# Products of the states with C, shared between VectorE and GpSimd in a fused state-space and attention kernel

## The chip, the cores and the metric

The kernel runs on one core of one Trainium2 chip. The metric is the device time of one launch in microseconds, as the median of several runs. A core has five engines that run side by side, each through its own instructions in order: TensorE (PE, matrix products), VectorE (DVE), ScalarE (ACT), GpSimd (POOL) and SyncE (SP). SP issues most of the DMAs; POOL issues those that add to what is there (`accum_op`), between its own arithmetic. The engines wait for one another by semaphores only.

## What is computed

Two layers over x of shape (2, 768, 64, 64), all in float32; the change lies in the first. Cut to what matters:

```python
xs = conv3x3_depthwise(in_proj(groupnorm(x)))        # 1536 channels, 9 taps
u = silu(xs)
dt, Bs, Cs = split(x_proj(u))                        # 48, 4 and 4 values a position
delta = softplus(dt_proj(dt) + dt_b)
dA  = exp(delta[..., None] * A)                      # 4 states a channel
dBu = (delta * u)[..., None] * Bs
s_t = dA_t * s_(t-1) + dBu_t                         # along all 4096 positions
y = sum_n(s_n * Cs_n) + D * u
out = out_proj(layernorm(y)); x = x + out
# second layer: attention over channels by heads, with two 768 x 768 products
```

## The kernel before, in words

The first layer works on tiles of 512 positions (8 rows of 64) by 128 channels: 16 tiles of positions (`NI`) with 12 chunks of channels each (`KI`), 192 pieces (`NQ0`), counted by g. The program is one loop over `step(g)`, in an order written out by hand (`tc.manual_schedule`); what stands first in a step's text is first in its engine's queue. One step works on several pieces at once: the input projection of piece n = g + 17, the convolution taps of piece a = g + 15 (`AHEAD`), the scan of piece g, the first sums of piece g - 1, the squares of g - 3, the output projection of the tile before (`BEHIND` = 12). A short fill comes before step 0, and the second layer (Strassen products and attention) after the last step.

The nine taps of the convolution are shared out. The middle one is ACT's (`tap_act`, line 412: it starts the sum `acc` in PSUM). `DMA_TAPS` (line 49) names those that ACT scales into `tm` buffers (line 427) and POOL's DMAs add up: `taps_dma_sum(a, q)` (line 433) adds the q-th buffer to the first, `taps_dma(a)` (line 439) adds the first to `u`. `PE_TAPS` (line 50) names those of TensorE, products with a diagonal matrix that ACT makes (`diag`, line 409; `taps_pe`, line 447). Both tuples are indexed by a % 4. What is left is DVE's (`taps_dve`, line 461): it reads the image from SBUF and `acc` from PSUM, and the last tap writes `u`.

For the scan of piece g, ACT makes `delta` for two pieces at a time, at odd g for g + 1 and g + 2 (`softplus_pair`, line 509), and four exponentials into `das[g % 2]` (`exps`, line 514). POOL multiplies delta by u (`du`, line 518, two buffers). DVE multiplies it by B for all four states into the single buffer `s` (line 537), runs the recurrence over the four states at once (line 539) and multiplies the states by C back into `das[g % 2]` (`times_c`, line 546). In the next step POOL adds states 0, 1 to states 2, 3 (`sum1`, line 526), and two DMAs add the two sums to `u`: `y_dma(g, 0)` one step after the scan, `y_dma(g, 1)` two steps after (line 533). ACT has by then multiplied u by D (line 530).

So a step in DVE's queue is: taps of a, product with B, scan, product with C. In POOL's queue it is: `sum1(g - 1)`, `du(g)`, the second tap sum of a, the two y DMAs, the tap sum of a + 1 and the tap DMA of a, and in one step of four two residual DMAs (`out_residual`, line 623). DVE also evicts the output projection in one step of four (line 615).

Of the kernel before, what the change touches and what calls it, by code (L numbers as in the profile page):

```python
# [19 lines left out]
NS = 4  # L20
# [14 lines left out]
NQ0 = NI * KI  # L35
# [11 lines left out]


DMA_TAPS = ((0, 2, 6), (0, 2, 6), (0, 2, 6), (0, 2))
PE_TAPS = ((), (1,), (), (1, 7))  # L50
FILL_DMA_TAPS = (0, 2)

AHEAD = 15
# [14 lines left out]
def both_layers(  # L68
# [225 lines left out]
    us, deltas, dus, sqs, tms = {}, {}, {}, {}, {}  # L294
# [90 lines left out]
    def dma_taps(a):  # L385
        return DMA_TAPS[a % 4] if a >= AHEAD else FILL_DMA_TAPS if a != KI - 1 else ()

    def pe_taps(a):
        return PE_TAPS[a % 4] if a > AHEAD else ()

# [41 lines left out]
    def taps_dma_sum(a, q):  # L432
        nc.gpsimd.dma_start(tms[a][0], tms[a][q], accum_op=ALU.add)  # L433
        if a < AHEAD:
            give(tms[a][q])

    def taps_dma(a):
        tm = tms.pop(a)[0]
        nc.gpsimd.dma_start(us[a], tm, accum_op=ALU.add)  # L439
        if a < AHEAD:  # L440
            give(tm)
# [52 lines left out]
    def load_bc(i, h):  # L494
        nc.sync.dma_start(bc[:, h * NS : (h + 1) * NS, :], bc_dr[i][h * NS : (h + 1) * NS, :].partition_broadcast(P))
# [15 lines left out]
    def exps(g):  # L511
        c = g % KI
        for n in range(NS):
            nc.scalar.activation(das[g % 2][:, n, 1:], deltas[g], AF.Exp, scale=neg_a[:, c, n : n + 1])  # L514

    def du(g):
        dus[g] = wk.tile([P, TL], F32, tag="du", name=f"du{g}")
        nc.gpsimd.tensor_mul(dus[g], deltas.pop(g), us[g])  # L518


    def ysums(g, n):
# [2 lines left out]
    def sum1(g):  # L524
        da = das[g % 2]
        nc.gpsimd.tensor_add(ysum[:, 0 : 2 + g % 2 : 1 + g % 2, :], da[:, 0:2, 1:], da[:, 2:4, 1:])  # L526
# [5 lines left out]
    def y_dma(g, n):  # L532
        nc.gpsimd.dma_start(us[g], ysums(g, n), accum_op=ALU.add)  # L533
# [8 lines left out]
        i, c, b, t = where(g)  # L542
        nc.scalar.copy(s[:, :, 0], state[c] if t else zeros[:, :NS])

    def times_c(g):
        nc.vector.tensor_mul(das[g % 2][:, :, 1:], s[:, :, 1:], bc[:, NS:, :])  # L546

    def state_out(g):
        i, c, b, t = where(g)
# [4 lines left out]
    def square(g):  # L554
        sqs[g] = wk.tile([P, TL], F32, tag="sq", name=f"sq{g}", bufs=3)
        nc.scalar.activation(sqs[g], us[g], AF.Square)
# [239 lines left out]
    lo, hi = slice(0, NH), slice(NH, QL)  # L796
# [358 lines left out]
    with tc.manual_schedule():  # L1155
# [31 lines left out]
        def step(g, prep=None, acts=None):  # L1187
            a, n = g + AHEAD, g + AHEAD + 2
            v = n
            do_b, do_c = 0 <= g < NQ0, BEHIND <= g < NQ0 + BEHIND  # L1190
# [95 lines left out]
            if 0 <= g - 3 < NQ0:  # L1286
                square(g - 3)

            if 0 <= g - 1 < NQ0:
                sum1(g - 1)  # L1290
            if do_b:
                du(g)
            late_tap = 0 <= a < NQ0 and len(dma_taps(a)) > 2
            if late_tap:
                taps_dma_sum(a, 2)
            if 0 <= g - 1 < NQ0:
                y_dma(g - 1, 0)
            if 0 <= g - 2 < NQ0:
                y_dma(g - 2, 1)
            if 0 <= a < NQ0 and dma_taps(a) and not late_tap:  # L1300
                taps_dma(a)
            if 0 <= a + 1 < NQ0 and dma_taps(a + 1):
                taps_dma_sum(a + 1, 1)
            if late_tap:
                taps_dma(a)
            if BEHIND < g <= NQ0 + BEHIND and (g - BEHIND) % 4 == 0:
                out_residual(g)
            if do_b:
# [11 lines left out]
            if 0 <= g + 1 < NQ0:  # L1320
                exps(g + 1)
            if do_b:
                state_out(g)
            if do_b:
                times_c(g)
                if g % KI == KI - 1 and g + 1 < NQ0:
                    load_bc(g // KI + 1, 1)
            if 0 <= g + 1 < NQ0:
# [24 lines left out]
        with tc.tile_pool(name="l0st", bufs=1, side="right") as sp:  # L1353
# [25 lines left out]
            for v in range(AHEAD + 1):  # L1379
                if 2 <= v < 6:  # L1380
                    out_weights_load(wg, 3 * (v - 2))
                step(first + v, lambda: products_of(v), lambda: scalar_of(v))
                if v == 0:
                    nc.scalar.activation(neg_a, pc[:, :, PC_A : PC_A + NS], AF.Exp)
                    nc.scalar.mul(neg_a, neg_a, -1.0)
                for k in scaled_w.get(v, ((), ()))[0]:
                    out_weights_sub(wg, wmean, k, nc.gpsimd)
                for k in scaled_w.get(v - 1, ((), ()))[1]:
                    out_weights_sub(wg, wmean, k, nc.vector)
                for k in sum(scaled_w.get(v - 1, ((), ())), ()):  # L1390
                    out_weights_store(wg, k)
# [8 lines left out]
        bc = late.tile([P, 2 * NS, TL], F32, name="bc")  # L1400
        s = late.tile([P, NS, TL + 1], F32, name="s")
# [4 lines left out]
        das = [late.tile([P, NS, TL + 1], F32, name="da0"), da1]  # L1406
        nc.gpsimd.memset(das[0][:, :, 0], 0.0)
        step(-1)
        nc.gpsimd.memset(das[1][:, :, 0], 0.0)
        for g in range(NQ0 + 2):  # L1410
            step(g)
# [68 lines left out]
@with_exitstack  # L1480
def mamba_then_attention(
    ctx, tc, x, in_wP, xp_wP, dt_wP, out_wT, pc_in, comb_in, pick_in, xsum_in, qkvP, woutP, temp_c, ident_in, gavg_in, gsel_in, hcol_in, hsel_in, esel_in, out
):
    nc = tc.nc
    keep = ctx.enter_context(tc.tile_pool(name="keep", bufs=1))
    dram = ctx.enter_context(tc.tile_pool(name="dram", bufs=1, space=DRAM))
    x1 = [dram.tile([DM, L], F32, name=f"x1_{b}") for b in range(NB)]

    stats1 = [keep.tile([P, KM, 2 * NT + 1], F32, name=f"stats1_{b}") for b in range(NB)]

    ident = keep.tile([P, P], F32, name="ident")
    nc.sync.dma_start(ident, ident_in)
    ones = keep.tile([P, P], F32, name="ones")
    nc.vector.memset(ones, 1.0)
    eps_c = keep.tile([P, 1], F32, name="eps_c")
    nc.vector.memset(eps_c, EPS)
    consts = (ident, ones, eps_c)


    wo_dr = dram.tile([KM // 2, KI // 3, P, 3, 2 * P], F32, name="wo_dr")  # L1500
    bc_dr = [dram.tile([2 * NS, TL], F32, name=f"bc_dr{i}") for i in range(NI)]

    s_dr = {k: dram.tile([KM // 2, 4, P, KM // 2, P], F32, name=f"s_dr_{k}") for k in ("p1", "p3")}
    both_layers(
        tc, nc, consts, x, in_wP, xp_wP, dt_wP, out_wT, pc_in, comb_in, pick_in, xsum_in, gavg_in, gsel_in, wo_dr, bc_dr, s_dr, x1, stats1,
        qkvP, woutP, temp_c, hcol_in, hsel_in, esel_in, [out[b].rearrange("c h w -> c (h w)") for b in range(NB)],
    )
# [105 lines left out]
```

## Time and profile before

| | us |
|---|---|
| median of three runs (3704.88 to 3710.76) | 3709.35 |
| span of the profiled execution | 3708.1 |
| PE busy in it | 3555.3 (96%) |
| DVE busy | 2842.1 (77%) |
| ACT busy | 2571.8 (69%) |
| POOL busy | 1782.8 (48%) |
| scan of one piece, L539, 192 times | 4.433 each, 851.1 in all |
| product with B, L537, 192 times | 2.288 each, 439.2 in all |
| DVE's taps, L461, 890 times | 0.753 and 0.748 each, 669.2 in all |
| delta times u, L518, 192 times | 1.284 each, 246.5 in all |
| PE's taps and their like, L447, 264 records | 140.0 in all |

The first scan starts 193.2 us into the span and the last at 2702.0, so a step takes 13.1 us on the average. The share of a whole span is an average over stages: DVE and ACT have little to do after 2700 us. PE does a product of 128x128 by 128x512 in float32 as two records. Lines of the profile carry the line of the kernel's text, the engine, the operation, the tile written and those read; in groups, the number after "x" is how often, then follow busy us, mean ns of one, and the engine's idle time just before them with what ended it. In answers in order of time the first two numbers are start and length in us.

### The profile page before, as it was taken

How to read it: one execution, taken by the hardware profiler on the slowest of the kernel's cores; microseconds unless marked ns; L12 is line 12 of the kernel's file. 1: busy time of each engine (PE TensorE's matmuls, PEld its weight loads, DVE VectorE, ACT ScalarE, POOL GpSimd, SP SyncE). 2: the span in 40 equal slices, each digit the busy share in tenths (PEclk: the TensorE clock that was granted, in tenths of full speed). 3: DMA queues.
4: the chain of work that ended last, by engine and by line, in shares of the span. 5: the costliest groups of instructions: out<-in, count | busy, mean ns of one | idle time of the engine just before them, and what ended most of it. 6: DMA issues, size and time to landing. Idle time of an engine off the chain costs nothing. (4 is left out here: it accounts for less than half of the span.)

```text
span 3708.1 us, 37935 instructions
## 1 busy us (share of the span) xinstructions
PE 3555.3 (96%) x11176; PEld 1771.0 (48%) x11176; DVE 2842.1 (77%) x2571; ACT 2571.8 (69%) x5026; POOL 1782.8 (48%) x1813
## 2 busy tenths in 40 slices
PE   5968999999999999999999999999999999999999
PEld 3423333343333333333344333433347658886688
DVE  7899999999999999999999999997721362224522
ACT  2688889888988898888888988897633542244221
POOL 0355565565655655555556655654443313330232
PEclk9978999999999999999999999999999999999999
DMA  9877888998989899898898989997676538763487
GB/s 354 232 169 162 182 204 185 205 211 191 212 176 209 201 200 208 184 204 185 187 203 194 212 175 211 203 201 177 142 202 183 192 93 265 256 205 123 158 268 245
DMA packets 380301, 738.98 MB, mean 199 GB/s; under 512 B 44304, under 2 KB 116944, under 8 KB 376000
## 3 DMA queue, kind: packets, MB, share of 16 engines
q0 software_dynamic: 146208, 270.08, 42.6%
q1 hardware_dynamic: 233888, 466.49, 38.4%
q8 instruction: 90, 1.47, 0.2%
q14 instruction: 115, 0.94, 0.1%
HBM read 440.96 MB, written 60.03 MB: 135 GB/s over the span
## 5 line engine op out<-in xcount | busy, mean ns | idle before, releaser
L362 PE MATMUL pa<-u,w 128*128 128x512 f32 (+1 forms) x2304 | 1035.8, 599 | 7.5 <-ACT carry L377 7.3
L603 PE MATMUL po<-u,w 128*128 128x512 f32 x2256 | 1011.5, 598 | 8.1 <-DVE u L615 7.9
L539 DVE TENSOR_TENSOR_SCAN s<-da,s 128x2052 f32<-128x2052 f32 x192 | 851.1, 4433 | 19.5 <-DVE s L537 0.9
L362 PEld LDWEIGHTS pa<-u,w 128*128 128x128 f32 x2304 | 429.5, 192 | 597.7 <-issue 484.7
L603 PEld LDWEIGHTS po<-u,w 128*128 128x128 f32 x2256 | 420.8, 190 | 582.7 <-issue 551.3
L526 POOL TENSOR_TENSOR ysum<-da 128x1024 f32<-128x1024 f32 x192 | 386.8, 2015 | 547.4 <-DVE da L546 464.1
L461 DVE SCALAR_TENSOR_TENSOR acc<-xs,pc,acc 128x512 f32<-128x512 f32 x698 | 525.6, 753 | 29.2 <-ACT acc L415 12.7
L537 DVE TENSOR_TENSOR s<-du,bc 128x2048 f32<-128x2048 f32 x192 | 439.2, 2288 | 83.0 <-POOL du L518 73.8
L433 POOL DMA_DIRECT2D tm<-tm x309 | 270.3, 875 | 462.7 <-ACT tm L427 423.5
L514 ACT ACTIVATE da<-dl,neg_a 128x512 f32<-128x512 f32 x768 | 489.6, 713 | 0.0
L546 DVE TENSOR_TENSOR da<-s,bc 128x2048 f32<-128x2048 f32 x192 | 440.0, 2292 | 6.3
L533 POOL DMA_DIRECT2D u<-ysum x384 | 380.4, 1255 | 4.2 <-issue 3.5
L427 ACT ACTIVATE tm<-xs,pc 128x512 f32<-128x512 f32 x486 | 317.1, 717 | 15.1 <-DMA tm<-tm 7.3
L415 ACT ACTIVATE acc<-xs,pc 128x512 f32<-128x512 f32 x192 | 132.2, 688 | 215.7 <-DVE u L461 206.4
L518 POOL TENSOR_TENSOR du<-dl,u 128x512 f32<-128x512 f32 x192 | 246.5, 1284 | 0.0
L439 POOL DMA_DIRECT2D u<-tm x177 | 206.1, 1164 | 59.6 <-issue 50.1
L447 PE MATMUL acc<-xs,dg 128*128 128x512 f32 x264 | 140.0, 641 | 50.0 <-ACT acc L415 49.6
L886 PE MATMUL po_p<-v,w 128*128 128x256 f32 x672 | 171.9, 380 | 1.4 <-ACT po_p L983 1.4
L886 PE MATMUL po_p<-u,w 128*128 128x256 f32 x624 | 159.7, 379 | 0.0
L461 DVE SCALAR_TENSOR_TENSOR u<-xs,pc,acc 128x512 f32<-128x512 f32 x192 | 143.6, 748 | 7.7
L831 POOL TENSOR_TENSOR v<-u 128x256 f32<-128x256 f32 x21 | 15.7, 758 | 277.1 <-ACT u L849 262.1
L886 PE MATMUL acc_p<-u,w 128*128 128x256 f32 x556 | 143.7, 382 | 4.6 <-DMA w<-woutP 3.4
(285 smaller groups left out, 5006.5 us busy)
## 6 DMA issues: line engine op xcount, KB each, us to landing
u<-ysum POOLq DMA_DIRECT2D x384, 256.0 KB, 5.5
tm<-tm POOLq DMA_DIRECT2D x309, 256.0 KB, 4.3
w<-in_wP SPq DMA_DIRECT2D x192, 384.0 KB, 4.4
w<-wo_dr SPq DMA_DIRECT2D x192, 384.0 KB, 4.7
u<-x SPq DMA_DIRECT2D x263, 256.0 KB, 4.8
w<-s_dr_p SPq DMA_DIRECT2D x288, 192.0 KB, 3.4
u<-tm POOLq DMA_DIRECT2D x177, 256.0 KB, 5.8
bc<-bc_dr SPq DMA_DIRECT2D x32, 1024.0 KB, 7.7
```

Of the source, the lines that this page charges most:

```text
L362: nc.tensor.matmul(pa[:, :nn], w[:, k, :], xts[i, k][:, :nn], start=(k == 0), stop=(k == KM - 1))
L427: nc.scalar.activation(tm.rearrange("p (h w) -> p h w", w=W), xs[:, dy : dy + TR, dx : dx + W], AF.Copy, scale=pc[:, c, PC_W + j : PC_W + ...
L433: nc.gpsimd.dma_start(tms[a][0], tms[a][q], accum_op=ALU.add)
L461: nc.vector.scalar_tensor_tensor(dst, xs[:, dy : dy + TR, dx : dx + W], pc[:, c, PC_W + j : PC_W + j + 1], acc, ALU.mult, ALU.add)
L514: nc.scalar.activation(das[g % 2][:, n, 1:], deltas[g], AF.Exp, scale=neg_a[:, c, n : n + 1])
L526: nc.gpsimd.tensor_add(ysum[:, 0 : 2 + g % 2 : 1 + g % 2, :], da[:, 0:2, 1:], da[:, 2:4, 1:])
L533: nc.gpsimd.dma_start(us[g], ysums(g, n), accum_op=ALU.add)
L537: nc.vector.tensor_mul(s[:, :, 1:], dus.pop(g).unsqueeze(1).to_broadcast([P, NS, TL]), bc[:, :NS, :])
L539: nc.vector.tensor_tensor_scan(sf, das[g % 2].rearrange("p n l -> p (n l)"), sf, 0.0, ALU.mult, ALU.add)
L546: nc.vector.tensor_mul(das[g % 2][:, :, 1:], s[:, :, 1:], bc[:, NS:, :])
L603: nc.tensor.matmul(po[e], w[:, kk, e * P : (e + 1) * P], us[i * KI + k], start=(k == 0), stop=(k == KI - 1))
L886: nc.tensor.matmul(dst, half[:, k, :], tiles[blocks[seq[i][0]][:3]][what][k], start=(start and k == 0), stop=(k == KH - 1), skip_group_che ...
```

## The change

The product with C is cut into two instructions of two states each: states 0 and 1 on GpSimd, at the end of POOL's step, states 2 and 3 on VectorE. `du` is computed one step sooner, for piece g + 1 behind the y DMAs. The second tap sum of a moves to the front of POOL's step, and `taps_dma(a)` always stands ahead of the tap sum of a + 1. TensorE keeps one tap in one chunk of four; the other two go to VectorE.

```diff
-PE_TAPS = ((), (1,), (), (1, 7))
+PE_TAPS = ((), (), (), (1,))
...
     def exps(g):
...
+        deltas.pop(g)
 
     def du(g):
         dus[g] = wk.tile([P, TL], F32, tag="du", name=f"du{g}")
-        nc.gpsimd.tensor_mul(dus[g], deltas.pop(g), us[g])
+        nc.gpsimd.tensor_mul(dus[g], deltas[g], us[g])
...
-    def times_c(g):
-        nc.vector.tensor_mul(das[g % 2][:, :, 1:], s[:, :, 1:], bc[:, NS:, :])
+    def times_c(g, engine, lo, hi):
+        engine.tensor_mul(das[g % 2][:, lo:hi, 1:], s[:, lo:hi, 1:], bc[:, NS + lo : NS + hi, :])
...
+            if 0 <= a < NQ0 and len(dma_taps(a)) > 2:
+                taps_dma_sum(a, 2)
             if 0 <= g - 1 < NQ0:
                 sum1(g - 1)
-            if do_b:
-                du(g)
-            late_tap = 0 <= a < NQ0 and len(dma_taps(a)) > 2
-            if late_tap:
-                taps_dma_sum(a, 2)
             if 0 <= g - 1 < NQ0:
                 y_dma(g - 1, 0)
             if 0 <= g - 2 < NQ0:
                 y_dma(g - 2, 1)
-            if 0 <= a < NQ0 and dma_taps(a) and not late_tap:
+            if 0 <= g + 1 < NQ0:
+                du(g + 1)
+            if 0 <= a < NQ0 and dma_taps(a):
                 taps_dma(a)
             if 0 <= a + 1 < NQ0 and dma_taps(a + 1):
                 taps_dma_sum(a + 1, 1)
-            if late_tap:
-                taps_dma(a)
...
             if do_b:
-                times_c(g)
+                times_c(g, nc.gpsimd, 0, NS // 2)
+                times_c(g, nc.vector, NS // 2, NS)
```

## The prediction

> **What bounds the kernel now.** I read the busy time by stage first, then the costliest groups, then DVE and POOL in order of time through one step, then every POOL tensor operation beside a DVE operation. In the scan stage (193 to 2707 us, 192 steps) two engines are full at once:
>
> ```profile
> 400.00:800.00 400.00, 394.86 (x1037) 156.69 (x1036) 386.15 (x247) 355.48 (x672) 237.16 (x221) 1.00 0.90 195
> 1200.00:1600.00 400.00, 395.12 (x1037) 157.22 (x1036) 386.26 (x246) 353.77 (x665) 237.19 (x221) 1.00 0.90 197
> ```
>
> The columns after the 400 us are PE, PEld, DVE, ACT and POOL: PE 98.7%, DVE 96.6%, ACT 89%, POOL 59%. So a saving on PE alone or DVE alone buys little, and POOL looks free. These rows give the prices (mean ns of one after the comma; the last two lines are issue to landing in us):
>
> ```profile
> L546 DVE TENSOR_TENSOR da<-s,bc 128x2048 f32<-128x2048 f32 x192 | 440.0, 2292 | 6.3
> L526 POOL TENSOR_TENSOR ysum<-da 128x1024 f32<-128x1024 f32 x192 | 386.8, 2015 | 547.4 <-DVE da L546 464.1
> L447 PE MATMUL acc<-xs,dg 128*128 128x512 f32 x264 | 140.0, 641 | 50.0 <-ACT acc L415 49.6
> tm<-tm POOLq DMA_DIRECT2D x309, 256.0 KB, 4.3
> u<-tm POOLq DMA_DIRECT2D x177, 256.0 KB, 5.8
> ```
>
> One step in order of time, DVE then POOL (start, length in us):
>
> ```profile
> 1516.91 4.43 DVE L539 TENSOR_TENSOR_SCAN s<-da,s 128x2052 f32<-128x2052 f32 x1
> 1521.38 2.29 DVE L546 TENSOR_TENSOR da<-s,bc 128x2048 f32<-128x2048 f32 x1
> 1523.59 2.33 DVE L461 SCALAR_TENSOR_TENSOR acc<-xs,pc,acc 128x512 f32<-128x512 f32 x3
> 1525.96 0.75 DVE L461 SCALAR_TENSOR_TENSOR u<-xs,pc,acc 128x512 f32<-128x512 f32 x1
> 1527.02 2.29 DVE L537 TENSOR_TENSOR s<-du,bc 128x2048 f32<-128x2048 f32 x1 [0.32 <-POOL du L518]
> ```
>
> ```profile
> 1522.12 1.20 POOL L439 DMA_DIRECT2D u<-tm  x1
> 1523.76 2.00 POOL L526 TENSOR_TENSOR ysum<-da 128x1024 f32<-128x1024 f32 x1 [0.43 <-DVE da L546]
> 1525.72 1.27 POOL L518 TENSOR_TENSOR du<-dl,u 128x512 f32<-128x512 f32 x1
> 1526.94 0.86 POOL L433 DMA_DIRECT2D tm<-tm  x1
> 1527.53 2.06 POOL L533 DMA_DIRECT2D u<-ysum  x2
> ```
>
> Both POOL tensor operations (3.2 us together) lie inside the stretch in which DVE does its taps L461, whose second tensor, acc, is in PSUM (line 414). POOL's DMA issues lie under the products and the scan. Through 192 steps no POOL tensor operation runs beside L537, L539 or L546, which read two SBUF tensors each; the scan's shortest, middle and longest are 4431, 4433 and 4434 ns. What happens when they meet is seen once, in the fill, where both engines subtract wmean from weights, all in SBUF:
>
> ```profile
> L287 DVE TENSOR_TENSOR wg<-wg,wmean x4: 943/946/6902, 151.6 to 171.8; 128x768 f32<-128x768 f32 x4
> 164.09 6.90 DVE L287 TENSOR_TENSOR wg<-wg,wmean 128x768 f32<-128x768 f32 x1
> 164.51 5.66 POOL L287 TENSOR_TENSOR wg<-wg,wmean 128x768 f32<-128x768 f32 x3
> ```
>
> A DVE operation of 0.946 us took 6.90 and ended 0.82 us after POOL's third (170.17): it stood still until POOL was through. So DVE operations with two SBUF tensors and POOL's tensor operations take turns; L461, with one, doesn't mind POOL.
>
> **The change part by part.** PE: the taps fall from 132 to 44 (264 records are 132 taps, issued 0.43 us apart), 88 x 0.86 = 76 us less PE, and 88 fewer diagonals on ACT (0.40 each, 35 us). DVE takes these taps: 88 x 0.79 (start to start) = 70 us more. DVE's product with C is halved: rows 768 wide at 0.946 and 2048 at 2.292 give 1.21 for 1024, so 192 x 1.08 = 207 us less. POOL gets 192 products 128x1024. No such product is in the trace; the nearest row is the sum L526 of the same size, 2.0 us, and the 512 to 768 rows (1.265, and 1.77 start to start) carried on give 2.3. I take 2.0 and keep 2.3 for the range: 384 us more POOL. The Trainium skill, "GPSIMD Engine Reference", section "Performance versus the Vector engine", has 4.5 us for twice the size; by it an estimate of 2.25 would stand here, 48 us more POOL over the stage, while the measured row for this size says 2.0.
>
> If nothing collides, DVE falls by 137 us, PE by 76, POOL rises to about 10.0 of 12.5 us a step (the 5.27 of tensor work summed below, 2.06 of y DMAs, 1.2 for the tap DMA, 0.55 for each of 1.75 tap sums, 0.5 for residuals), and PE remains the bound.
>
> But they collide. **Turns in one step:** DVE 2.29 + 4.43 + 1.21 = 7.93; POOL 2.0 + 2.0 + 1.27 = 5.27; together 13.2 us. That alone exceeds the 12.9 us of an ordinary step (2.21 product, 3.83 five taps, 2.39 product, 4.47 scan, start to start). Before, the same sum was 9.01 + 3.28 = 12.3, and POOL's part hid entirely under taps. Now POOL's 5.27 us face 3.8 us of taps.
>
> The order of the queues makes it worse. Put zero at the end of scan(g); I assume that whoever has asked gets the turn when one ends. *Good step:* DVE's half 0 to 1.2 (it follows its scan by 0.04, POOL wakes about 0.1 after), POOL's half 1.2 to 3.2, issue of the second tap sum to 3.8, sum L526 3.8 to 5.8. DVE's taps end at 5.0, its product waits until 5.8 and ends 8.1. POOL's two y DMAs end at about 7.8, du asks in time and slips in at 8.1 to 9.4, the scan runs 9.4 to 13.9. Period 13.9.
>
> *Bad step:* du missed that gap and waits out the scan. Then du 0 to 1.3, DVE's half to 2.5; behind du in POOL's queue are the tap DMA (1.2) and the first tap sum (0.55), so POOL's half runs 3.0 to 5.0. The second tap sum waits for the first to land, 4.3 after its issue at 2.5, so L526 asks at 7.4. DVE's taps end 6.3, its product 8.6, then L526 8.6 to 10.6, scan to 15.1. Period 15.1, and du, behind L526 and 2 us of DMAs, misses again: the bad step repeats itself. It is left in the chunk with two DMA taps (one in four), where L526 needs no second sum. It is entered where delta is late: at odd g, du(g+1) needs the softplus of that same step, which in the trace ends 8.0 us after a scan's end (1516.5 against 1508.46), just where the gap is. I take three bad steps to one good: (3 x 15.1 + 13.9) / 4 = 14.8, 1.9 over 12.9, times 192 = 365 us.
>
> The other moves cost nothing beside this. du a step sooner removes the waits of L537 for it (73.8 us in total, 71 times), but DVE then waits for its turn instead; the tap DMA now comes 5 us and more after the sum that it needs (4.3); the residual's two DMAs (2.1 us, one step in four) are hidden under the scan in a good step and move POOL's half by 2.1 in a bad one. PE's 76 us and ACT's 35 come off engines that then wait.
>
> Sum: 3708 + 365 = 4073 us, against the profiled execution's span; the median of the runs, 3709, is 1 us off.
>
> On who gets the turn, the row first: DVE's L287 began by its record 0.42 us before POOL's first, and still waited for all three, so POOL, once in, kept on. The Trainium skill, "SBUF — State Buffer", section "Who interferes with whom", has an exclusive lock held for one whole instruction, the first to issue winning, between a DVE instruction with two SBUF inputs and a GpSimd one that reads SBUF. It speaks against this change; by it the turns above alternate (4073), by the row read strictly POOL's half and L526, back to back in one chunk of four, would shut DVE out for 4.0 us at a stretch, which the bad step without a second sum holds already.
>
> **Rivals.** *A, the scan isn't subject to turns* (no run of it beside POOL is in this trace, and L287 is a plain product of two tensors), or the halves hardly meet. Then du and the sum hide under the 4.4 us scan, and the step is 1.2 + 3.8 + 0.8 + 2.3 + 4.5 = 12.6, what PE needs without its taps. Time 3708 - 76 = 3632, faster. Against it: the scan reads da and s from SBUF, as L287 does its two. It decides from a scan that stays 4.43 beside POOL. *B, DVE keeps its turn* from product through scan to half, because they follow within 0.04 to 0.10 us. Then L526 and du wait up to 8 us, POOL's half starts 3 us after that, and the next product waits for it: some 17 us a step, 4.1 x 192 = 787, 4495 us. For it: the gaps are short; against it: at 164 us POOL got in although DVE's record had begun. *C, good steps throughout:* 1.0 x 192, 3900 us, if the softplus always comes in time (in the trace it is 0.1 us inside); with DVE's evictions (1.4 us, one step in four) as more cover, some 3860.
>
> **How the numbers follow.** Forecast with its mixture of steps 0.62, C 0.18, B 0.06, A 0.12, no measurable change 0.02. Bounds of the forecast: bad steps alone 2.2 x 192 = 422, 4130; with the residual's 2.1 us exposed in one of four, another 101, 4231. Below: C at 3860 and the floor of turns packed without a gap, 13.2 against 12.9, 58 us, 3766. So 3780 to 4240 leaves out A, B and the no-change case, 0.20. A measurement of this kernel tells 0.2% (7 us). Faster is A, 0.12; same 0.02; slower 0.86.
>
> **What would show it.** Right: L538, L540 and the halved L547 on DVE lengthen from 2.29, 4.43 and 1.2 by whole POOL operations, du or L526 recorded or started only after a scan's end, DVE busy on paper while it stands still, PE's share down to about 85%, steps near 14 and 15. Wrong: scans of 4.43 beside a running POOL product, and PE still at 98%.

## The result, and the profile after

The changed kernel takes 3927.2 us (median of four runs, 3920.4 to 3936.9) against 3709.9 for the kernel before on the same chip: a ratio of 1.0593, 95% interval 1.0575 to 1.0611, 217 us slower. The forecast was slower, 4073 us, with a range of 3780 to 4240. The profiled execution has a span of 3918.6 us. The scan stage alone, from the first scan to the last, grew from 2508.8 to 2725.8 us, 13.14 to 14.27 a step; what lies after the last scan took 1002 us before and 995 now.

The costliest groups of the changed kernel on the two engines of the change; after the bar busy us, mean ns of one, then idle time before them:

```profile
L540 DVE TENSOR_TENSOR_SCAN s<-da,s 128x2052 f32<-128x2052 f32 x192 | 1058.5, 5513 | 19.5 <-ACT xs L374 0.5
L547 POOL TENSOR_TENSOR da<-s,bc 128x1024 f32<-128x1024 f32 x192 | 594.1, 3094 | 224.7 <-DVE s L540 211.4
L538 DVE TENSOR_TENSOR s<-du,bc 128x2048 f32<-128x2048 f32 x192 | 549.8, 2864 | 43.4 <-POOL da L547 34.1
L519 POOL TENSOR_TENSOR du<-dl,u 128x512 f32<-128x512 f32 x192 | 507.1, 2641 | 2.7 <-ACT dl L509 2.7
L527 POOL TENSOR_TENSOR ysum<-da 128x1024 f32<-128x1024 f32 x192 | 484.6, 2524 | 7.6 <-DMA u<-ysum 1.8
L547 DVE TENSOR_TENSOR da<-s,bc 128x1024 f32<-128x1024 f32 x192 | 298.3, 1554 | 6.3
```

The instructions of the scan, of the product with B and of du are the same as before, but their mean went from 4433 to 5513 ns, from 2288 to 2864 and from 1284 to 2641: standing still is now written into the durations, not into the idle times. VectorE and POOL hold each other up here inside instructions that have already begun, so what stands ahead of the prediction, that engines wait for one another by semaphores only, does not hold for these two. On VectorE the scan is 207 us longer in all, the product with B 111, the taps 66 (978 of them, not 890), and the product with C is 142 shorter instead of the 205 that half of it is worth (192 x 1.225 would be 235). That is 242 us more. Between the first scan and the last VectorE is busy for 2619 us instead of 2370, 249 more, and idle for 107 instead of 139, 32 less (the waits ahead of the product with B alone fell from 83 to 43): the 217 us.

The busy time by stage (PE, PEld, DVE, ACT, POOL, then granted clock, DMA share, GB/s):

```profile
400.00:800.00 400.00, 363.13 (x910) 143.02 (x910) 384.99 (x243) 318.61 (x592) 323.92 (x232) 0.94 0.82 179
1200.00:1600.00 400.00, 364.87 (x928) 144.08 (x928) 390.39 (x244) 319.16 (x597) 320.33 (x229) 0.96 0.85 188
```

TensorE fell from 98.7% to 91%, its granted clock from 1.00 to about 0.95; VectorE reads 97%, a good part of it waiting. One step in order of time, VectorE first:

```profile
1528.92 5.41 DVE L540 TENSOR_TENSOR_SCAN s<-da,s 128x2052 f32<-128x2052 f32 x1
1534.37 1.23 DVE L547 TENSOR_TENSOR da<-s,bc 128x1024 f32<-128x1024 f32 x1
1535.51 3.12 DVE L461 SCALAR_TENSOR_TENSOR acc<-xs,pc,acc 128x512 f32<-128x512 f32 x4
1538.73 0.75 DVE L461 SCALAR_TENSOR_TENSOR u<-xs,pc,acc 128x512 f32<-128x512 f32 x1
1539.39 3.25 DVE L538 TENSOR_TENSOR s<-du,bc 128x2048 f32<-128x2048 f32 x1
```

```profile
1528.10 1.93 POOL L519 TENSOR_TENSOR du<-dl,u 128x512 f32<-128x512 f32 x1
1529.91 0.96 POOL L439 DMA_DIRECT2D u<-tm  x1
1531.08 0.86 POOL L433 DMA_DIRECT2D tm<-tm  x1 [0.20 <-issue]
1534.42 3.22 POOL L547 TENSOR_TENSOR da<-s,bc 128x1024 f32<-128x1024 f32 x1 [2.48 <-DVE s L540]
1537.58 0.85 POOL L433 DMA_DIRECT2D tm<-tm  x1
1538.19 2.29 POOL L527 TENSOR_TENSOR ysum<-da 128x1024 f32<-128x1024 f32 x1
```

Every meeting of the two engines is there. du asks at 1528.10, while the product with B runs, gets in as that ends and holds the scan up: 5.41 instead of 4.43. POOL's half starts 0.05 us behind VectorE's, waits for its 1.2 us and takes 3.22. The sum takes its turn at 1538.19, so the product with B, which asks at 1539.39, reads 3.25 instead of 2.29. From scan to scan it is 13.8 us. This is the good step of the forecast (13.9), meeting by meeting. The other kind:

```profile
1085.33 6.06 DVE L540 TENSOR_TENSOR_SCAN s<-da,s 128x2052 f32<-128x2052 f32 x1
1091.42 2.12 DVE L547 TENSOR_TENSOR da<-s,bc 128x1024 f32<-128x1024 f32 x1
```

```profile
1084.80 2.30 POOL L527 TENSOR_TENSOR ysum<-da 128x1024 f32<-128x1024 f32 x1
1087.39 1.76 POOL L534 DMA_DIRECT2D u<-ysum  x2 [0.30 <-POOL ysum L527]
1088.53 3.94 POOL L519 TENSOR_TENSOR du<-dl,u 128x512 f32<-128x512 f32 x1
```

Here the sum gets in ahead of the scan (6.06), du finds the scan running, waits to its end (3.94) and holds up VectorE's half (2.12 instead of 1.22). This is the bad step.

The trace also shows what opens bad steps. They come in 24 stretches of one or more, and in 16 of these POOL stood, right before the sum of the first bad step, at the second tap sum until the first had landed, for 1.5 to 3.6 us; so the sum came after the product with B had begun and, all but once, went in ahead of the scan. In one of the 24 du waited for delta. Between 400 and 2400 us this wait for a landing is (us in total, times, longest)

```profile
POOL tm L433 <- DMA tm<-tm: 61.7, 31, 3.6
```

where the kernel before has 12.8 us in all. 20 of the 24 stretches end at the chunk with two DMA taps, as the prediction has it.

### The profile page after: what moved, and what is told of

It is laid out like the page before. It is cut to its first block, busy times and chain, and to the rows that moved or that the text cites. A ratio compares the mean times of both kernels' runs of the same rounds, so it can differ in the third digit from the quotient of the medians.

```text
span 3918.6 us, 37975 instructions
## 1 busy us (share of the span) xinstructions
PE 3569.3 (91%) x11000; PEld 1767.1 (45%) x11000; DVE 3091.7 (79%) x2659; ACT 2561.0 (65%) x4938; POOL 2553.6 (65%) x2005
## 5 line engine op out<-in xcount | busy, mean ns | idle before, releaser
L604 PE MATMUL po<-u,w 128*128 128x512 f32 x2256 | 1091.7, 637 | 187.5 <-DVE u L616 187.4
L540 DVE TENSOR_TENSOR_SCAN s<-da,s 128x2052 f32<-128x2052 f32 x192 | 1058.5, 5513 | 19.5 <-ACT xs L374 0.5
L547 POOL TENSOR_TENSOR da<-s,bc 128x1024 f32<-128x1024 f32 x192 | 594.1, 3094 | 224.7 <-DVE s L540 211.4
L461 DVE SCALAR_TENSOR_TENSOR acc<-xs,pc,acc 128x512 f32<-128x512 f32 x786 | 591.8, 753 | 33.3 <-ACT acc L415 13.6
L538 DVE TENSOR_TENSOR s<-du,bc 128x2048 f32<-128x2048 f32 x192 | 549.8, 2864 | 43.4 <-POOL da L547 34.1
L519 POOL TENSOR_TENSOR du<-dl,u 128x512 f32<-128x512 f32 x192 | 507.1, 2641 | 2.7 <-ACT dl L509 2.7
L527 POOL TENSOR_TENSOR ysum<-da 128x1024 f32<-128x1024 f32 x192 | 484.6, 2524 | 7.6 <-DMA u<-ysum 1.8
L433 POOL DMA_DIRECT2D tm<-tm x309 | 313.1, 1013 | 206.1 <-DMA tm<-tm 84.4
L534 POOL DMA_DIRECT2D u<-ysum x384 | 338.6, 1023 | 68.0 <-POOL ysum L527 57.6
L547 DVE TENSOR_TENSOR da<-s,bc 128x1024 f32<-128x1024 f32 x192 | 298.3, 1554 | 6.3
```

What stands on the lines that cost most here:

```text
L461: nc.vector.scalar_tensor_tensor(dst, xs[:, dy : dy + TR, dx : dx + W], pc[:, c, PC_W + j : PC_W + j + 1], acc, ALU.mult, ALU.add)
L519: nc.gpsimd.tensor_mul(dus[g], deltas[g], us[g])
L538: nc.vector.tensor_mul(s[:, :, 1:], dus.pop(g).unsqueeze(1).to_broadcast([P, NS, TL]), bc[:, :NS, :])
L540: nc.vector.tensor_tensor_scan(sf, das[g % 2].rearrange("p n l -> p (n l)"), sf, 0.0, ALU.mult, ALU.add)
L547: engine.tensor_mul(das[g % 2][:, lo:hi, 1:], s[:, lo:hi, 1:], bc[:, NS + lo : NS + hi, :])
L604: nc.tensor.matmul(po[e], w[:, kk, e * P : (e + 1) * P], us[i * KI + k], start=(k == 0), stop=(k == KI - 1))
```

## The experiments

Each is the kernel before, or the changed one, with one or two edits. The kernel before beside them took 3706 to 3711 us. Intervals are 95% of the ratio to it.

**taps_alone.** One line of the change:

```diff
-PE_TAPS = ((), (1,), (), (1, 7))
+PE_TAPS = ((), (), (), (1,))
```

> The kernel before with the taps of the change alone: 88 taps go from TensorE to VectorE. Theory of turns (two-SBUF operations of VectorE and POOL's tensor operations take turns; the lost time of the change lies in the product with B and in the scan): here POOL's work stays under the taps, so the only cost is that steps of four taps (12.5 us) become steps of five (12.9): 88 x 0.4 = 35 us, about 3745. Rival, the taps explain the loss: the whole 70 us of them or more, 3780 and up. Rival, TensorE was the bound: 76 us less, down to 3634.

3759.9 us, ratio 1.0135 (1.0117 to 1.0152): 52 us for 88 taps, 0.6 each, between the two sizes. TensorE was not the bound in the sense of the rival: taking 76 us off it gave nothing. The scan stays at 4.433 throughout. The taps are a small part of the loss.

**split_alone.** The kernel before, with the product with C cut as in the change, du and the order as before:

```diff
...
-                times_c(g)
+                times_c(g, nc.gpsimd, 0, NS // 2)
+                times_c(g, nc.vector, NS // 2, NS)
```

> The kernel before with the product with C split between the engines alone; du stays behind the sum, old taps and order. Theory of turns: after the scan's end VectorE's half to 1.2, POOL's half to 3.2, the sum to 5.2, du to 6.45, then the product with B, against 6.04 (five taps) or 5.6 (four) before: 0.4 to 0.85, about 0.6 x 192 = 120, 3830; the scan rows stay 4.43. Rival, VectorE gains its 207 us and POOL is free: 3500 to 3640.

3817.0 us, ratio 1.029 (1.0273 to 1.0307), as the turns have it. Scan and product with B, from the groups of its profile:

```profile
L539 DVE TENSOR_TENSOR_SCAN s<-da,s 128x2052 f32<-128x2052 f32 x192 | 851.1, 4433 | 19.4 <-ACT sq L556 0.5
L537 DVE TENSOR_TENSOR s<-du,bc 128x2048 f32<-128x2048 f32 x192 | 440.0, 2292 | 370.9 <-POOL du L518 355.6
```

No scan is touched, but the 205 us that VectorE saves turn into a wait of 371 for du (83 before), which now stands behind POOL's half and the sum. The median step is 13.47 us, where the working said 13.3.

**du_alone.** The changed kernel with the old taps and the whole product with C on VectorE, so that du's place and the new order of the tap DMAs are left:

```diff
-PE_TAPS = ((), (), (), (1,))
+PE_TAPS = ((), (1,), (), (1, 7))
...
-                times_c(g, nc.gpsimd, 0, NS // 2)
-                times_c(g, nc.vector, NS // 2, NS)
+                times_c(g, nc.vector, 0, NS)
```

> The kernel before with delta times u a step sooner and the new order of POOL's DMAs, no split, old taps. Theory of turns: du now falls between the product with B and the scan, and the scan rows read about 5.4 instead of 4.43 in most steps; the sum L527 hides under the taps as before. 1.0 a step, less 0.3 in the steps of four taps that waited for du: some 0.8 x 192 = 155, about 3865. Rival, no turns for the scan: the wait for du (73.8 us) goes, 3636 to 3709, scans of 4.43.

3936.0 us, ratio 1.061 (1.0587 to 1.0633). The direction is that of turns (median scan 5.32 us), but it is 71 us over the expectation, as slow as the whole change. So two further runs took du's place and the place of the second tap sum apart. The third move, `taps_dma(a)` ahead of the tap sum of a + 1, has no run of its own.

**du_place_alone.** The kernel before with du for g + 1 behind the y DMAs:

```diff
...
-            if do_b:
-                du(g)
...
                 y_dma(g - 2, 1)
+            if 0 <= g + 1 < NQ0:
+                du(g + 1)
```

> The kernel before with delta times u a step sooner, behind the y DMAs, and nothing else: the second tap sum stays behind the sum, the tap DMA last. Theory of turns: du meets the scan, whose rows read 5.3 to 5.4 in most steps; 0.98 a step, less 0.3 in steps of four taps, 0.8 x 192 = 155: 3865. If the order of the tap sums made all of du_alone's loss, and turns none, 3640 to 3709 and scans of 4.43.

3960.7 us, ratio 1.0681 (1.0659 to 1.0702): worse than with the new order. The expectation named the wrong victim. The median scan is 4.433; it is the product with B that is hit. VectorE, then POOL, in order of time:

```profile
1515.45 4.32 DVE L538 TENSOR_TENSOR s<-du,bc 128x2048 f32<-128x2048 f32 x1
1519.88 4.43 DVE L540 TENSOR_TENSOR_SCAN s<-da,s 128x2052 f32<-128x2052 f32 x1
```

```profile
1514.26 2.06 POOL L534 DMA_DIRECT2D u<-ysum  x2
1515.36 2.26 POOL L519 TENSOR_TENSOR du<-dl,u 128x512 f32<-128x512 f32 x1
```

du, 0.09 us ahead of the product, begins by its record before POOL has done with the second DMA issue (1516.32), ends 1.30 after that, and keeps VectorE waiting for 2.0 us: the product takes 4.32 instead of 2.29. An operation of 1.27 us cost 2.0: by these records it had its turn while POOL still issued the DMA. The DMA issue alone does not hold VectorE: in the kernel before 190 products with B and 166 scans have one beside them, and none is longer than 2.295 or 4.434 us.

**order_alone.** The kernel before with the second tap sum ahead of the sum:

```diff
+            if late_tap:
+                taps_dma_sum(a, 2)
             if 0 <= g - 1 < NQ0:
                 sum1(g - 1)
             if do_b:
                 du(g)
-            if late_tap:
-                taps_dma_sum(a, 2)
```

> The kernel before with one thing changed: the second tap sum stands ahead of the sum L526 in POOL's queue, with its wait for the first one to land. If this order is a cost of its own, the sum and du behind it come up to 2.6 us later in three chunks of four (first sum issued at 1521.6 in the trace of before, landed 4.3 later, against 1523.8 for the sum) and the product with B waits for du: 200 to 370 us more, 3910 to 4080, with scans of 4.43 throughout. If only turns between the engines cost, and not the order, 3709.

3872.5 us, ratio 1.0439 (1.0419 to 1.0459): 162 us, a cost of its own, somewhat under the expected 200 to 370, and no scan above 4.435. The wait, from the table of waits between 400 and 2400 us (us in total, times, longest):

```profile
POOL tm L433 <- DMA tm<-tm: 310.4, 78, 8.0
```

POOL stands there until the first sum has landed, the sum and du come later, and the product with B waits for du: 240 us of idle time in its group (83 before).

**s2_back.** The changed kernel with that order undone, `sum1(g - 1)` ahead of `taps_dma_sum(a, 2)`:

> The changed kernel with the second tap sum back behind the sum; split, du a step sooner and taps as in the change. If the order costs beside the turns, the sum now asks right behind POOL's half (3.2 instead of 3.8 and later): 0.6 a step in three of four and the steps in which the sum came after the product with B go, 90 to 150 us less than the change, 3780 to 3840. If du only slides from in front of the scan to its end, and blocks VectorE's half there, nothing is gained: 3900 to 3930.

3862.8 us, ratio 1.0419 (1.0397 to 1.0441): 64 us better than the change, less than the 90 to 150, since the median scan is now 5.92: the sum comes in time, and du, right behind the y DMAs, meets the scan instead (152 scans beside du alone). VectorE's halves that were blocked, the mark of the bad step, fall from 68 to 38. Of the change's 217 us the place of the second tap sum holds 64.

**du_back.** The changed kernel with `du(g)` directly behind `sum1(g - 1)`:

> The changed kernel with delta times u back behind the sum, for piece g; split, taps and the order of the tap DMAs as in the change. If turns are what is lost, the place of du does not save them: POOL's half to 3.2, second tap sum to 3.8, sum to 5.8, du to 7.05, the product with B then, scan of 4.43: 13.9 in three chunks of four, 13.45 in the fourth, against 13.84 of the changed kernel; some 3870, all lost time now idle time of VectorE ahead of the product with B. If the collision of du with the scan were a loss of its own, its removal would give back 1 us a step: 3740.

3996.1 us, ratio 1.0777 (1.0759 to 1.0795): slower than the change, so within it the early du saves 69 us, and the rival's 3740 is out. Scan, product with B and du by its groups:

```profile
L539 DVE TENSOR_TENSOR_SCAN s<-da,s 128x2052 f32<-128x2052 f32 x192 | 851.2, 4433 | 19.4 <-ACT xs L374 0.5
L537 DVE TENSOR_TENSOR s<-du,bc 128x2048 f32<-128x2048 f32 x192 | 440.1, 2292 | 493.8 <-POOL du L518 464.5
L518 POOL TENSOR_TENSOR du<-dl,u 128x512 f32<-128x512 f32 x192 | 281.8, 1468 | 0.0
```

The loss has moved into 494 us of idle time ahead of the product with B. The median step is 14.24 us, not 13.9: behind a DMA issue the sum takes 2.30 us instead of 2.0, and from its start to du's end it is 3.52 us instead of 3.23 (the two records overlap).

**du_no_read.** The changed kernel with du filled, not computed:

```diff
-        nc.gpsimd.tensor_mul(dus[g], deltas[g], us[g])
+        nc.gpsimd.memset(dus[g], 0.01)
```

> The changed kernel, but du is filled with a constant by POOL at the same place: delta times u is left out, the instruction still writes 128x512 to SBUF and reads nothing. If it is POOL's reading that takes turns with VectorE, the scan rows go back to 4.43 and a step from 13.8 to about 12.7, 3919 - 1.05 x 192 = some 3720. If any POOL operation takes turns, the scan is still longer by the length of the fill, 3780 to 3850. If du is not what lengthens the scan, 3920.

3813.9 us, ratio 1.0281 (1.0246 to 1.0315). The time alone fits the second reading; the rows give the first. A fill and the scan beside it, and then all scans (shortest, middle, longest in ns):

```profile
1306.40 4.43 DVE L540 TENSOR_TENSOR_SCAN s<-da,s 128x2052 f32<-128x2052 f32 x1
```

```profile
1305.56 1.18 POOL L519 MEMSET du<- 128x512 f32 x1
```

```profile
L540 DVE TENSOR_TENSOR_SCAN s<-da,s x192: 4432/4433/7009, 194.8 to 2790.9; 128x2052 f32<-128x2052 f32 x192
```

The 74 scans beside a fill alone all took 4.432 to 4.434 us. The long ones, 59 of 6.04 us and more, all had the sum beside them. So a write alone takes no turn. The Trainium skill, "SBUF — State Buffer", section "Who interferes with whom", says the same: contention with a GpSimd instruction that reads SBUF, not with one that only writes it. As to the 94 us over the expected 3720, scans are still 106 us longer in all than undisturbed, products with B 101 and VectorE's halves 26, and every lengthened one has the sum beside it.

**du_one_read.** The changed kernel with du from one tensor:

```diff
-        nc.gpsimd.tensor_mul(dus[g], deltas[g], us[g])
+        nc.gpsimd.tensor_scalar_mul(dus[g], us[g], 0.01)
```

> The changed kernel with du computed from u and a constant, so with one SBUF input instead of two: delta is left out. If one input is enough for a turn, the scans beside it are still lengthened, by the shorter time of this operation (some 0.5 to 1.0 us), and the time is between du_no_read's 3814 and the change's 3927. If it takes two inputs, scans read 4.43 as in du_no_read, 3814.

3936.1 us, ratio 1.0616 (1.0595 to 1.0637), not below the change as expected. One input is enough: 99 scans beside this du alone have a middle of 4.74 us, 0.31 over the undisturbed, against 5.39 (108 scans) beside the two-input du; VectorE's halves beside it take 1.45 us, against 2.11. But the operation with a scalar is itself no shorter on POOL (1.49 us at the least, against 1.27). What the scans gained, 88 us in all, came back for the most part as idle time ahead of the product with B, 115 us instead of 43.

**no_half** and **half_no_read.** The changed kernel without POOL's half, and with a fill in its place:

```diff
-                times_c(g, nc.gpsimd, 0, NS // 2)
+                nc.gpsimd.memset(das[g % 2][:, : NS // 2, 1:], 0.01)
```

> The changed kernel without POOL's half of the product with C: states 0 and 1 are not multiplied by C. By turns: VectorE's half to 1.2, the sum to 3.2 hidden under the taps (to 5.05), du still beside the scan (5.4): 12.9 a step instead of 13.84, some 3745. If POOL's half is hidden where it is, 3920.

> The changed kernel with POOL's half replaced by a fill of the same 128x2x512 elements, which reads nothing: states 0 and 1 are not multiplied by C. If only POOL's reading takes turns, the fill runs beside VectorE's half from the end of the scan and is done soon after it; the sum is hidden again: close to no_half, 3745 to 3800. If writing takes turns too, or POOL's queue is the limit, near 3920.

3857.4 us, ratio 1.0404 (1.0383 to 1.0424), and 3872.5, ratio 1.0445 (1.0424 to 1.0465). They lie 15 us apart, so the fill is nearly free, and 118 halves of VectorE beside it alone took 1.217 to 1.228. But both give back only 55 to 70 us of the 130 to 180 expected. The waits of no_half between 400 and 2400 us show why:

```profile
POOL tm L433 <- DMA tm<-tm: 272.4, 64, 8.0
```

In the change this wait is 61.7 us. With POOL free sooner, the second tap sum, now first in its queue, waits for the landing, and the sum behind it comes when the product with B or the scan already runs: scans have a middle of 5.39 us again. POOL's half partly hides a wait that the order makes.

**more_pe.** The kernel before with the taps moved the other way:

```diff
-PE_TAPS = ((), (1,), (), (1, 7))
+PE_TAPS = ((), (1,), (1,), (1, 7))
```

> The kernel before with the taps moved the other way: one more chunk of four gives a tap to TensorE, 44 taps off VectorE. taps_alone cost 0.6 us for each tap moved to VectorE (52 us for 88). If VectorE's queue is the bound, 44 x 0.4 to 0.6 = 18 to 26 us less, 3684 to 3692. If TensorE, at 98.7% of the scan stage, is as much the bound, its 44 x 0.86 = 38 us more eat that up: 3709 to 3730. A version that beats both kernels only in the first case.

3710.1 us, ratio 1.0001 (0.9992 to 1.0010): no change. Its stage:

```profile
400.00:800.00 400.00, 399.63 (x1052) 160.08 (x1051) 381.10 (x239) 357.29 (x681) 236.71 (x221) 1.00 0.90 196
```

TensorE is full to 99.9%, VectorE down to 95.3%: what one gained the other lost. No version tried beats the kernel before.

## Why the prediction was right, and where its sizes were off

- *Direction and mechanism.* VectorE's operations with two SBUF tensors and POOL's tensor operations take turns. The prediction read that from one row of the fill (0.946 us became 6.90) and carried it over to products and scan. It holds: undisturbed 4.43, beside a two-input du 5.39, beside du and sum 6.05 and more; beside a fill 4.43. Rival A, a scan that knows no turns, is refuted by the first row of the page after.
- *The good step*, 13.9 worked out: the 123 steps without a blocked half have a middle of 13.81.
- *The bad step*, 15.1 worked out: the other 68 have a middle of 14.34. The term that failed is the price of a turn. Each waiting was charged with POOL's whole operation, 2.0 and 1.27; the rows show 1.62 for the sum (6.05 against 4.43) and 0.89 for du (2.11 against 1.22). The difference, 0.38 twice, is the 0.76 us between 15.1 and 14.34.
- *The mixture*, three bad to one good, failed too: it is 68 bad of 191. Against the same steps of the kernel before, a good step is 0.96 us longer in the mean (1.0 forecast) and a bad one 1.48 (2.2 forecast): 118 and 101 us, about the 217 measured. The forecast's sizes with the measured mixture would give 274 us, the measured sizes with the forecast's mixture 259, instead of 365: the two errors weigh about alike. Rival C, good steps throughout, with 3900, lay closest, but a third of the steps are not good.
- *How a bad step is entered* was wrong. It was to be entered where softplus comes late; in the trace du waits for ACT 2.7 us in all, once, and the way in is the late landing of the first tap sum ahead of the second (16 of 24 times). The prediction had that wait inside the bad step, as a consequence. Why delta was not late was not tested; that the steps are longer than before, and ACT with them less busy (80% in place of 89%), is the likely reason.
- *Rival B*, VectorE keeping its turn across the gaps of 0.10 us, is out: the sum and du get in there.
- *POOL's product* was taken at 2.0 us, with 2.3 as the other end. Its shortest row is 2.17; the middle, 3.21, begins with VectorE's half and ends 2.0 behind it. The estimate of 2.25 by the Trainium skill, "GPSIMD Engine Reference", section "Performance versus the Vector engine", is nearer to the shortest row; the 2.0 of the sum's row is what a half behind VectorE's takes.
- *What was costed at nothing.* The new place of the second tap sum was: alone it costs 162 us and within the change 64. So was du's place, which alone costs 250. The taps, 70 us in the working, cost 52 alone; TensorE's 76 us were worth nothing, as said.
- The parts do not add up: 52 + 109 + 162 + 250 is 573, and together, with the move of `taps_dma(a)`, they cost 217. du's early place costs 250 in the kernel before and saves 69 in the changed one. Where POOL's operations already overflow the taps, an operation that meets the scan replaces a wait elsewhere; that this is all of the difference was not shown.

## What to carry to other kernels

An engine that looks half idle can still be unable to take work: ask not only for its busy share but which of its operations can run beside which of the other engine's. Here work moved from VectorE to POOL cost more turns (13.2 us a step by the prediction's sum) than the step had time (12.9), and none of the places in the queue that were tried made it free. Move what reads no SBUF, or keep the two engines' SBUF-reading work under operations of the other that take their second tensor from PSUM, as the kernel before does.

## What the runs showed of the hardware that was not expected

- By the records a POOL operation can take its turn while POOL still issues a DMA, and then costs more than its own length: du, 1.27 us of work right behind the y DMAs, held VectorE's product up for 2.0 us in the step shown of du_place_alone, and the median scan of s2_back for 1.49 (5.92 against 4.43).
- A POOL operation that found VectorE's operation running and waited for its end costs VectorE about 0.4 us less than its own length (1.62 for 2.0, 0.89 for 1.27).
- A one-input POOL operation (1.49 us long at the least) lengthens the scan by 0.31 us and VectorE's half by 0.22, a two-input one of the same 512 elements by 0.96 and 0.89, a fill by nothing.
- VectorE's taps, whose second tensor is in PSUM, do not wait for POOL: in the kernel before 712 of them beside a POOL tensor operation have a middle of 0.755 us, 178 others 0.750.
